# Norms and weight casts moved from VectorE to ScalarE, low parts to GpSimd, in an SSM block with a gated feed-forward part

## The chip, the cores and the metric

The kernel runs on one core of a Trainium2 chip. A core has TensorE (PE, with its weight loads, PEld, listed apart), VectorE (DVE), ScalarE (ACT), GpSimd (POOL) and SyncE (SP), which here only issues DMAs. The metric is the device time of one execution in microseconds. Before the change it is 608.14 us, the median of three runs (607.9 to 608.25).

## The reference

The input is x of shape (4, 512, 256): four batches of 512 tokens. Both halves of the block normalize x, scale and shift it by factors made from a small conditioning vector, and add their gated result to x.

```python
mod = (silu(c) @ wmod).reshape(4, 6, 1, 256)      # sa, ca, ga, sb, cb, gb
h = layernorm(x) * (1 + ca) + sa
x = x + ga * attn(h)
h = layernorm(x) * (1 + cb) + sb
x = x + gb * ffn(h)

# attn: a state-space layer, 32 heads of 8 channels, state 64, written as masked attention
proj = u @ W_in.T                                  # 4640 columns: x, B, C | z | A_log
xBC = causal_conv4(xBC) + conv_b                   # per channel, 4 taps
Lm = exp(segsum(-softplus(A_log)))                 # lower triangular decay
M = einsum('blhn,bshn,bhls->bhls', C, B, Lm)
y = einsum('bhls,bshp->blhp', M, x) + D * x
out = y * silu(z + z_bias) @ W_out.T

# ffn
hidden = fwht(silu(x @ W1.T) * (x @ W3.T))         # Walsh-Hadamard transform, 1024 wide
out = hidden @ W2.T
```

## The kernel before

**Split products.** The large products are done on float32 values held as two parts in a format of TensorE (F32R): a high part, which is the value cast to that format, and a low part, the value minus the high part. A projection (`proj`) is six matmuls, high by high, low by high and high by low, over two halves of the 256 inputs. So each weight that is loaded is split by `split`: one cast for the high part, one subtraction on POOL for the low part. The transposed activations are split in `modulate`: ACT makes the high part from PSUM, DVE makes the full value `hf` from PSUM, and a subtraction (L292) makes the low part.

**Stages.** The first part goes over eight units, two halves `i` of the heads by four batches `b`: all batches of half 0, and then of half 1. A unit has eight steps `k` (64 in all), two groups of four called `m`. Each step projects B and C for two heads (`project`: `bc` and `cc`), puts each through `conv`, builds the decay factors `l` (`prep_l`), multiplies them with the products of B and C (`attend`, L446), and transposes B (`turn_b`). For each `m`, states are summed over chunks of 64 tokens (`states`, `turn_states` with the scan L550), and `intra` and `inter` give the output. At the end of a unit comes the gate; after half 1 of a batch also the output projection, the second norm (`normalize(b, 1, ...)`, `modulate(b, 1, ...)`) and a spill of its result to memory. The feed-forward part then runs over 32 steps, eight per batch (`up`, `down`).

**One convolution.** `conv` reads a projection from PSUM in four passes: two on ACT (L375 with the fourth tap and the bias, L377 with the first tap into `cv`), two on DVE (L378, L379), and it ends with an addition on POOL (L380). The projection's PSUM tile, one of three (`ps_p`), is free once ACT and DVE have read it.

**A norm.** `normalize` takes x as four tiles of 128 tokens by 256: per tile `bn_stats` and `bn_aggr` on DVE (L269, L270), then variance plus epsilon on DVE (L271), a power of -0.5 on POOL (L272, `rs`), and four `tensor_scalar` on DVE that subtract the mean and multiply with `rs` (L274, `xn`). `xn` has a single buffer. PE transposes it (L284) for `modulate`. The first norm of a batch is part 0 of `prologue`, its `modulate` is part 1; part 2 makes the decay sums from `hf`, which the masks `dr` and `dl` are loaded from.

**The order of work.** Python runs an agenda: each function has a due time in steps (`T`), and functions are put into the program in the order of these times. For batches 1 to 3, part 0 of `prologue` is due 11.83 steps, part 1 7.06 steps ahead of the batch's first unit. SP's queue keeps that order. For the other engines, the framework plans the order when the program is built, by a simulation of times (`schedule_with_timeline_sim=True`), and may put an instruction ahead of others that come before it in the program. `with tc.issue_after(ins)` keeps what is made inside it, on the engine of `ins`, behind `ins`; `behind(...)` does this with the last instruction noted in `last` under each name given. [...] Three places make weight splits ahead of the loop (`split_quad`, `split_xz`), others in the loop (`load_quad`, `xz1`, `load_ffn`).

Of the kernel before, what the change touches and what calls it, by code (L numbers as in the profile page):

```python
# [13 lines left out]
F32 = mybir.dt.float32  # L14
F32R = mybir.dt.float32r
BF16 = mybir.dt.bfloat16
AF = mybir.ActivationFunctionType
ALU = mybir.AluOpType
# [3 lines left out]
NB, S, DM = 4, 512, 256  # L22
# [8 lines left out]
def mamba_ffn(tc, ctx, u, c_t, wmod, win_t, cw, cb, zb, dsk, wo_t, w13_t, w2_t,  # L31
              k_ident, k_reset, k_dl, k_dr, k_had, k_own, out):
    nc = tc.nc
    ve, ac, gp, pe = nc.vector, nc.scalar, nc.gpsimd, nc.tensor
# [17 lines left out]
    def after(dt, fn, *args):  # L52
        at_time(now[0] + dt, fn, *args)
# [6 lines left out]
    def work(shape, name, tag, bufs=2, dtype=F32):  # L60
        return wk.tile(shape, dtype, name=name, tag=tag, bufs=bufs)

    def mtile(shape, name):
        return ps_m.tile(shape, F32, name=name, tag="m")
# [4 lines left out]
    def load_x(which, b, src, step=4):  # L69
        t = work([128, 4, DM], f"x{which}{b}", "x", 1)  # L70
        for n in range(0, 4, step):
            nc.sync.dma_start(t[:, n : n + step], src[:, n : n + step])
        return t

    def tok_rows(ap):
        return ap.rearrange("(t p) d -> p t d", p=128)

    x_in = {0: load_x(0, 0, tok_rows(u[0]), 2)}
# [88 lines left out]
            ts.append(t)  # L167
        return ts

    def split(dst, c0, width, ts):  # L170

        for k, t in enumerate(ts):
            d = dst[:, :, k, c0 : c0 + width]
            ve.tensor_copy(d[:, 0], t)
            gp.tensor_tensor(d[:, 1], t, d[:, 0].bitcast(F32), ALU.subtract)

    wa = const.tile([128, 2, 32], F32, name="wa")
# [1 line left out]
    wxz = {}  # L179
    wo = const.tile([128, 2, 2, DM], F32R, name="wo")  # L180
    wq = {}
# [1 line left out]
    def fetch_quad(n, half, **kw):  # L183
        return fetch(win_t[:, 544 + 1024 * n : 544 + 1024 * n + 1024], 512 * half, 512, f"wq{n}", **kw)

    def split_quad(n, half, ts):
        if half == 0:
            wq[n] = work([128, 2, 2, 1024], f"wq{n}", "wq", 2, F32R)
        split(wq[n], 512 * half, 512, ts)

    def load_quad(n, half):
        split_quad(n, half, fetch_quad(n, half))
# [1 line left out]
    def fetch_xz(i, **kw):  # L194
        return fetch(win_t[:, 256 * i : 256 * i + 256], 0, 256, f"wxz{i}", **kw)

    def split_xz(i, ts):
        wxz[i] = work([128, 2, 2, 256], f"wxz{i}", "wxz", 1, F32R)
        split(wxz[i], 0, 256, ts)

    def load_wo():
        for k in range(2):
# [41 lines left out]
    last = {}  # L244
# [12 lines left out]
    def behind(*engines):  # L257
        stack = ExitStack()
        for e in engines:
            stack.enter_context(tc.issue_after(last[e].ins))  # L260
        return stack

    def normalize(b, which, x):
        mv = work([128, 4, 2], f"mv{which}{b}", "mv")
        rs = work([128, 4], f"rs{which}{b}", "rs")
        xn = work([128, 4, DM], f"xn{which}{b}", "xn", 1)
        for t in range(4):
            bs = work([128, 6], f"bs{which}{b}{t}", "bs")
            ve.bn_stats(bs, x[:, t])  # L269
            ve.bn_aggr(mv[:, t], bs)  # L270
        ve.tensor_scalar(rs, mv[:, :, 1], EPS, None, ALU.add)  # L271
        last[gp] = gp.tensor_tensor(rs, rs, neghalf, ALU.pow)  # L272
        for t in range(4):
            ve.tensor_scalar(xn[:, t], x[:, t], mv[:, t, 0:1], rs[:, t : t + 1], ALU.subtract, ALU.mult)  # L274
        return xn

    def modulate(b, which, xn):

        sh = [msc[:, 4 * which + k, b : b + 1] for k in range(2)]
        scl = [msc[:, 4 * which + 2 + k, b : b + 1] for k in range(2)]  # L280
        pts = [mtile([128, S], f"pt{which}{b}{k}") for k in range(2)]
        for t in range(4):
            for k in range(2):
                pe.transpose(pts[k][:, 128 * t : 128 * t + 128], xn[:, t, 128 * k : 128 * k + 128], ident)  # L284
        full = [work([128, S], f"hf{which}{b}{k}", "hf") for k in range(2)]
        hts = [work([128, 2, S], f"ht{which}{b}{k}", "ht", 6, F32R) for k in range(2)]
        ac.activation(hts[0][:, 0], pts[0], AF.Identity, bias=sh[0], scale=scl[0])
        for k in (1, 0):
            ve.tensor_scalar(full[k], pts[k], scl[k], sh[k], ALU.mult, ALU.add)
        ac.activation(hts[1][:, 0], pts[1], AF.Identity, bias=sh[1], scale=scl[1])  # L290
        for k in range(2):
            last[ve] = ve.tensor_tensor(hts[k][:, 1], full[k], hts[k][:, 0].bitcast(F32), ALU.subtract)  # L292
        return full, hts

    def spill(name, tiles):
# [16 lines left out]
    xns, fulls, phss, dfs = {}, {}, {}, {}  # L312

    def prologue(b, part, fill=None):
        if part == 0:
            if b not in x_in:
                x_in[b] = load_x(0, b, tok_rows(u[b]))
            xns[b] = normalize(b, 0, x_in.pop(b))
        elif part == 1:
            fulls[b], ht[0, b] = modulate(b, 0, xns.pop(b))  # L320
            htd[b] = spill(f"htd{b}", ht[0, b])
        elif part == 2:

            full = fulls.pop(b)
            pa = mtile([128, 128], f"pa{b}")
            for k in range(2):
                for t in range(4):
                    last[pe] = pe.matmul(pa[32 * t : 32 * t + 32], wa[:, k], full[k][:, 128 * t : 128 * t + 128],
                              start=(k == 0), stop=(k == 1), skip_group_check=True, tile_position=(0, 32 * t))
            e = work([128, 128], f"spe{b}", "spe", 1)  # L330
            at = work([128, 128], f"at{b}", "at", 1)
            ac.activation(e, pa, AF.Abs)
            last[ve] = ve.tensor_scalar(at, pa, 0.0, -1.0, ALU.max, ALU.mult)
            if fill:
                fill()
            ac.activation(e, e, AF.Exp, scale=-1.0)
            ac.activation(e, e, AF.Ln, bias=1.0)
            ve.tensor_tensor(at, at, e, ALU.subtract)
            phs = phss[b] = work([128, 128], f"phs{b}", "phs", 1)
            ve.tensor_tensor_scan(phs, reset, at, 0.0, ALU.mult, ALU.add)  # L340

            parts = work([128, 3, 128], f"parts{b}", "parts", 1, BF16)
            rest = work([128, 128], f"rest{b}", "at", 1)
            ve.tensor_copy(parts[:, 0], phs)
            ve.tensor_tensor(rest, phs, parts[:, 0], ALU.subtract)
            ve.tensor_copy(parts[:, 1], rest)
            last[ve] = ve.tensor_tensor(parts[:, 2], rest, parts[:, 1], ALU.subtract)
            p_dr3[b] = dram.tile([NH, 3, S], BF16, name=f"p3{b}")
            p_dr[b] = dram.tile([NH, S], F32, name=f"pd{b}")
            p_end[b] = dram.tile([NH, NC], F32, name=f"pend{b}")  # L350
            for t in range(4):
                (gp if T["p3gp"] and b == 0 and t % 2 else nc.sync).dma_start(p_dr3[b][:, :, 128 * t : 128 * t + 128], parts[32 * t : 32 * t + 32])
            after(1, write_sums, b, phs)
        elif part == 3:

            phs = phss.pop(b)
            df = dfs[b] = work([128, 128], f"df{b}", "df", 1)
            p_c = phs.rearrange("p (c l) -> p c l", l=Q)
            ve.tensor_tensor(df.rearrange("p (c l) -> p c l", l=Q), p_c[:, :, Q - 1 :].to_broadcast([128, 2, Q]),
                             p_c, ALU.subtract)  # L360
            ac.activation(df, df, AF.Exp)
        else:
            pw = mtile([128, 128], f"pw{b}")
            pe.transpose(pw, dfs.pop(b), ident)
            wdec[b] = const.tile([128, 4, NH], F32, name=f"wd{b}")
            ac.activation(wdec[b].rearrange("p t h -> p (t h)"), pw, AF.Copy)
# [6 lines left out]
    def conv(ps, tl, dst):  # L373
        w = cw_sb[:, tl]
        ac.activation(dst, ps, AF.Identity, bias=cb_sb[:, tl : tl + 1], scale=w[:, 3:4])  # L375
        v = work([128, S], "cv", "cv", 3)
        last[ac] = ac.activation(v, ps, AF.Copy, scale=w[:, 0:1])  # L377
        ve.scalar_tensor_tensor(dst[:, 1:], ps[:, : S - 1], w[:, 2:3], dst[:, 1:], ALU.mult, ALU.add)  # L378
        ve.scalar_tensor_tensor(dst[:, 2:], ps[:, : S - 2], w[:, 1:2], dst[:, 2:], ALU.mult, ALU.add)  # L379
        last[gp] = gp.tensor_tensor(dst[:, 3:], dst[:, 3:], v[:, : S - 3], ALU.add)  # L380

    units = [(i, b) for i in range(2) for b in range(NB)]
# [258 lines left out]
    q00 = fetch_quad(0, 0, **early)  # L641
    fxz = fetch_xz(0, **early)
    q01 = fetch_quad(0, 1, **early)
    q10 = fetch_quad(1, 0, **early)
    q11 = fetch_quad(1, 1)
    with behind(gp):
        split_quad(0, 0, q00)
    prologue(0, 1)
    with behind(gp):
        for t in sts:  # L650
# [3 lines left out]

    def split_more():
        with behind(gp, ve):
            split_xz(0, fxz)
            split_quad(0, 1, q01)

    prologue(0, 2, split_more)  # L660
    load_d(0)
    for k in range(AHEAD):
        for half in range(2):
            with behind(pe, ve):
                project(k, half)
        if k == 1:
            with behind(gp, ve):
                split_quad(1, 0, q10)
    with behind(pe):
        x_proj(0)  # L670
    with behind(gp, ve):
        split_quad(1, 1, q11)
    prologue(0, 3)
    with behind(pe):
# [204 lines left out]
```

## Time and profile before

| | |
|---|---|
| median of 3 runs | 608.14 us |
| profiled execution: own time, span | 611.31 us, 609.4 us |
| mean granted clock of TensorE | 0.976 |
| busy PE, DVE, ACT, POOL | 549.5, 454.3, 367.5, 314.9 us |
| xn (L274), DVE | 32 instructions, 17.7 us |
| low parts of activations (L292), DVE | 16 instructions, 13.4 us |
| casts of weights (L174), DVE | 28 instructions, 17.2 us |
| `fh` (L693), ACT, 128x512 from SBUF into F32R | 32 instructions, mean 632 ns |
| `fl` (L694), POOL, 128x512 from SBUF into F32R | 31 instructions, mean 1294 ns |

Busy times of a group are unions: two instructions that overlap count once, while a mean is of single durations. A line with an arrow at its end, such as [1.87 <-DVE bc L379], says that the engine stood idle for 1.87 us just before and that the named instruction released it. The stages in what follows are start-up (0 to 20 us), the ramp of the first unit (20 to 60), the loop over the units (to about 475), and the feed-forward part, whose first steps begin inside the end of the loop.

### The profile page before, as it was taken

To read this page: it belongs to the slowest core of one execution; us is meant where nothing else is said; L and a number is where in the kernel's file an instruction comes from. 1 tells how busy PE (TensorE), PEld (TensorE's weight loads), DVE (VectorE), ACT (ScalarE), POOL (GpSimd) and SP (SyncE) were. 2 spreads that over 40 slices of the span, in tenths; PEclk is the share of its full clock that TensorE was granted. 3 is DMA by queue.
4 is the path that set the end of the run, shared out by engine and by line. 5 is a ranking of instruction groups with operands and counts; after the bars stand their busy time and mean duration, and the time that the engine had idled before them with its cause. 6 is when DMAs were issued, how large, how long until landed. Compare 5 with 4: busy or idle time off the path is not lost. (4 is left out here: it accounts for less than half of the span.)

```text
span 609.4 us, 16345 instructions
## 1 busy us (share of the span) xinstructions
PE 549.5 (90%) x6836; PEld 435.8 (72%) x6836; DVE 454.3 (75%) x820; ACT 367.5 (60%) x600; POOL 314.9 (52%) x288
## 2 busy tenths in 40 slices
PE   3777898899889979999999899979979999999996
PEld 3554676678667756676777576757857888888886
DVE  5978798897796879889879888989888384343342
ACT  5657678867867765697785678567643233322221
POOL 5564243644534476764655558456576545325341
PEclk9978999999889989999999999999988999999999
DMA  6331111020313305201501244145139033304021
GB/s 199 107 127 70 40 37 72 10 67 3 105 27 101 110 2 164 92 3 58 170 4 37 75 131 146 58 131 176 37 119 298 9 124 117 125 0 147 1 78 36
DMA packets 42113, 52.00 MB, mean 85 GB/s; under 512 B 18230, under 2 KB 30260, under 8 KB 42040
## 3 DMA queue, kind: packets, MB, share of 16 engines
q1 hardware_dynamic: 40504, 50.54, 26.2%
q8 instruction: 54, 0.88, 0.6%
q10 hardware_dynamic: 1472, 0.38, 0.3%
q14 instruction: 19, 0.16, 0.1%
q0 software_dynamic: 64, 0.05, 0.0%
HBM read 33.51 MB, written 17.44 MB: 84 GB/s over the span
## 5 line engine op out<-in xcount | busy, mean ns | idle before, releaser
L380 POOL TENSOR_TENSOR cc<-cc,cv 128x509 f32<-128x509 f32 x64 | 70.5, 1101 | 75.2 <-DVE cc L379 69.7
L380 POOL TENSOR_TENSOR bc<-bc,cv 128x509 f32<-128x509 f32 x64 | 71.3, 1114 | 58.0 <-DVE bc L379 34.5
L242 PE MATMUL f<-h,wf 128*128 128x512 f32 x384 | 98.3, 396 | 0.0
L242 PEld LDWEIGHTS f<-h,wf 128*128 128x128 f32 x384 | 69.4, 191 | 12.3
L694 POOL TENSOR_TENSOR fl<-ft,fh 128x512 fp32r<-128x512 f32 x31 | 40.1, 1294 | 64.1 <-ACT fh L693 60.7
L375 ACT ACTIVATE cc<-pcc,cb_sb,cw_sb 128x512 f32<-128x512 f32 x64 | 49.8, 778 | 26.5 <-PE pcc L242 15.0
L375 ACT ACTIVATE bc<-pbc,cb_sb,cw_sb 128x512 f32<-128x512 f32 x64 | 50.0, 781 | 24.7 <-PE pG L255 15.2
L242 PE MATMUL pcc<-ht,wq 128*128 128x512 f32 x192 | 55.7, 428 | 10.0 <-DVE bc L379 8.1
L378 DVE SCALAR_TENSOR_TENSOR cc<-pcc,cw_sb,cc 128x511 f32<-128x511 f32 x64 | 47.4, 741 | 20.9 <-ACT cv L377 19.9
L242 PE MATMUL pbc<-ht,wq 128*128 128x512 f32 x192 | 56.7, 432 | 5.5 <-DVE cc L379 4.0
L693 ACT ACTIVATE fh<-ft 128x512 fp32r<-128x512 f32 x32 | 20.2, 632 | 66.9 <-PE pdyi L701 36.8
L689 DVE SCALAR_TENSOR_TENSOR ft<-ft,f 128x512 f32<-128x512 f32 x32 | 21.9, 687 | 49.6 <-ACT ft L688 45.4
L242 PE MATMUL pcc<-hr,wq 128*128 128x512 f32 x192 | 52.1, 405 | 3.0 <-ACT cv L377 1.5
L242 PE MATMUL pbc<-hr,wq 128*128 128x512 f32 x192 | 51.7, 404 | 2.2 <-DVE cc L379 2.0
L242 PEld LDWEIGHTS pcc<-ht,wq 128*128 128x128 f32 x192 | 37.4, 202 | 20.4 <-DVE bc L379 4.1
L454 ACT ACTIVATE bt<-bT 128x512 f32<-128x512 f32 x64 | 38.6, 604 | 19.6 <-PE bT L452 19.5
L378 DVE SCALAR_TENSOR_TENSOR bc<-pbc,cw_sb,bc 128x511 f32<-128x511 f32 x64 | 47.3, 740 | 3.0 <-ACT cv L377 3.0
L242 PEld LDWEIGHTS pbc<-ht,wq 128*128 128x128 f32 x192 | 37.2, 203 | 17.3 <-DVE cc L379 1.9
L379 DVE SCALAR_TENSOR_TENSOR bc<-pbc,cw_sb,bc 128x510 f32<-128x510 f32 x64 | 47.4, 741 | 1.2
L379 DVE SCALAR_TENSOR_TENSOR cc<-pcc,cw_sb,cc 128x510 f32<-128x510 f32 x64 | 47.4, 741 | 1.1
L452 PE MATMUL bT<-ident,bc 128*128 128x128 f32 x256 | 41.8, 286 | 3.9 <-DVE cc L379 1.2
L377 ACT ACTIVATE cv<-pcc,cw_sb 128x512 f32<-128x512 f32 x64 | 43.7, 683 | 2.0 <-POOL bc L380 2.0
(148 smaller groups left out, 1237.0 us busy)
## 6 DMA issues: line engine op xcount, KB each, us to landing
wq<-win_t SPq DMA_DIRECT2D x16, 256.0 KB
htd<-ht SPq DMA_DIRECT2D x8, 512.0 KB
hr<-htd SPq DMA_DIRECT2D x8, 512.0 KB
h2d<-ht SPq DMA_DIRECT2D x8, 512.0 KB
h<-h2d SPq DMA_DIRECT2D x8, 512.0 KB
x<-u SPq DMA_DIRECT2D x7, 512.0 KB
ex<-pd SPq DMA_DIRECT2D x8, 256.0 KB
ygd<-yg SPq DMA_DIRECT2D x4, 512.0 KB
```

What stands on the lines that cost most here:

```text
L242: last[pe] = pe.matmul(ps, w[:, a, k, c0 : c0 + 128], ht[k][:, b], start=(n == 0), stop=(n == 5))
L375: ac.activation(dst, ps, AF.Identity, bias=cb_sb[:, tl : tl + 1], scale=w[:, 3:4])
L377: last[ac] = ac.activation(v, ps, AF.Copy, scale=w[:, 0:1])
L378: ve.scalar_tensor_tensor(dst[:, 1:], ps[:, : S - 1], w[:, 2:3], dst[:, 1:], ALU.mult, ALU.add)
L379: ve.scalar_tensor_tensor(dst[:, 2:], ps[:, : S - 2], w[:, 1:2], dst[:, 2:], ALU.mult, ALU.add)
L380: last[gp] = gp.tensor_tensor(dst[:, 3:], dst[:, 3:], v[:, : S - 3], ALU.add)
L452: pe.transpose(pt[:, t], bc[:, 128 * t : 128 * t + 128], ident)
L454: ac.activation(bts[k], pt, AF.Copy)
L689: ve.scalar_tensor_tensor(t, t, 1.0, p1, ALU.add, ALU.mult)
L693: ac.activation(hi, t, AF.Copy)
L694: (ve if (b, f) == (NB - 1, 7) else gp).tensor_tensor(lo, t, hi.bitcast(F32), ALU.subtract)
```

## The change

Four edits:

1. `split` casts on ACT unless it is told to use DVE. The first half quad, the first `xz` and the second half quad (six casts) stay on DVE; the other 22 go to ACT. The two later splits of the start-up are kept behind `last[ac]`, the last `cv` pass, where they were kept behind `last[ve]`.
2. `normalize` makes `xn` on ACT with a scale `rs` and a bias `nm`, which is minus the mean times `rs`, made by one more small instruction on DVE. The first norm (batch 0) stays as it was.
3. `modulate` makes the low parts on POOL, but for batch 0's first.
4. The statistics of the first norms of batches 1 to 3 are kept behind the second DVE pass of the last convolution put into the program before them. This holds for what runs on DVE, since the noted instruction is on DVE.

```diff
-    def split(dst, c0, width, ts):
+    def split(dst, c0, width, ts, e=ac):
         for k, t in enumerate(ts):
             d = dst[:, :, k, c0 : c0 + width]
-            ve.tensor_copy(d[:, 0], t)
+            if e is ac:
+                ac.activation(d[:, 0], t, AF.Copy)
+            else:
+                ve.tensor_copy(d[:, 0], t)
             gp.tensor_tensor(d[:, 1], t, d[:, 0].bitcast(F32), ALU.subtract)
...
         last[gp] = gp.tensor_tensor(rs, rs, neghalf, ALU.pow)
+        if (b, which) == (0, 0):
+            for t in range(4):
+                ve.tensor_scalar(xn[:, t], x[:, t], mv[:, t, 0:1], rs[:, t : t + 1], ALU.subtract, ALU.mult)
+            return xn
+        nm = work([128, 4], f"nm{which}{b}", "nm")
+        ve.scalar_tensor_tensor(nm, mv[:, :, 0], -1.0, rs, ALU.mult, ALU.mult)
         for t in range(4):
-            ve.tensor_scalar(xn[:, t], x[:, t], mv[:, t, 0:1], rs[:, t : t + 1], ALU.subtract, ALU.mult)
+            ac.activation(xn[:, t], x[:, t], AF.Identity, bias=nm[:, t : t + 1], scale=rs[:, t : t + 1])
         return xn
...
+        e = ve if (which, b) == (0, 0) else gp
         for k in range(2):
-            last[ve] = ve.tensor_tensor(hts[k][:, 1], full[k], hts[k][:, 0].bitcast(F32), ALU.subtract)
+            last[e] = e.tensor_tensor(hts[k][:, 1], full[k], hts[k][:, 0].bitcast(F32), ALU.subtract)
...
-            xns[b] = normalize(b, 0, x_in.pop(b))
+            with behind(*(["conv"] if b else [])):
+                xns[b] = normalize(b, 0, x_in.pop(b))
...
-        ve.scalar_tensor_tensor(dst[:, 2:], ps[:, : S - 2], w[:, 1:2], dst[:, 2:], ALU.mult, ALU.add)
+        last["conv"] = ve.scalar_tensor_tensor(dst[:, 2:], ps[:, : S - 2], w[:, 1:2], dst[:, 2:], ALU.mult, ALU.add)
...
     with behind(gp):
-        split_quad(0, 0, q00)
+        split_quad(0, 0, q00, ve)
...
         with behind(gp, ve):
-            split_xz(0, fxz)
-            split_quad(0, 1, q01)
+            split_xz(0, fxz, ve)
+            split_quad(0, 1, q01, ve)
...
-            with behind(gp, ve):
+            with behind(gp, ac):
                 split_quad(1, 0, q10)
...
-    with behind(gp, ve):
+    with behind(gp, ac):
         split_quad(1, 1, q11)
```

## The prediction

> **What bounds the kernel now.** I read the busy times of the page, cut them into stages with the busy time by stretch, asked which PE gaps end on VectorE in each stage, and then read the timeline around the long gaps. The page first (busy us, share of the span, instructions):
>
> ```profile
> PE 549.5 (90%) x6836; PEld 435.8 (72%) x6836; DVE 454.3 (75%) x820; ACT 367.5 (60%) x600; POOL 314.9 (52%) x288
> ...
> PE 27%; DVE 12%; DMA 3%; POOL 2%; issue 1%; ACT 1%; SPq 0%; DVEq 0%; POOLq 0%
> ```
>
> The second line is the chain that ended last. It reaches back only to 328 us, and its PE share is mostly the feed-forward part at the end; before 475 us DVE is its largest member. By stage (length, then busy PE, PEld, DVE, ACT, POOL, the granted clock and DMA):
>
> ```profile
> 20.00:60.00 40.00, 28.18 (x181) 20.04 (x182) 34.39 (x69) 25.88 (x43) 21.64 (x21) 0.87 0.24 82
> 60.00:200.00 140.00, 128.06 (x2007) 97.48 (x2008) 116.33 (x220) 106.14 (x176) 60.48 (x57) 0.98 0.17 50
> 200.00:260.00 60.00, 53.46 (x853) 40.93 (x853) 50.51 (x84) 40.86 (x68) 39.22 (x35) 0.97 0.29 93
> ...
> 320.00:475.00 155.00, 141.93 (x2046) 109.31 (x2044) 134.68 (x251) 97.14 (x160) 94.00 (x84) 0.98 0.38 120
> 475.00:609.40 134.40, 129.05 (x808) 114.15 (x807) 55.33 (x91) 37.29 (x61) 53.31 (x43) 0.99 0.22 71
> ```
>
> From 475 us the kernel is PE alone (129.05 of 134.4). From 20 to 475 us (260 to 320 is not shown: PE 58.48, DVE 50.44, ACT 48.11, POOL 34.34) PE is busy 410.1 of 455, DVE 386.4 (85%), ACT 318.1 (70%), POOL 249.7 (55%). PE idles 45 us there, and by its waits in each stage some 34 us of these end on DVE. The operations that the change moves stand in those gaps. Timeline, DVE and PE:
>
> ```profile
> 31.42 4.84 DVE L274 TENSOR_SCALAR xn<-x,mv,rs 128x256 f32<-128x256 f32 x4
> ...
> 42.22 0.75 DVE L269 BATCH_NORM_STATS2 bs<-x 128x6 f32<-128x256 f32 x2 [3.08 <-DMA x<-u]
> ...
> 212.44 1.45 DVE L174 CAST wq<-wq 128x512 fp32r<-128x512 f32 x1 [0.18 <-DMA wq<-win_t]
> ...
> 214.60 2.84 PE L242 MATMUL pcc<-ht,wq 128*128 128x512 f32 x6 [1.87 <-DVE bc L379]
> ...
> 450.44 0.43 DVE L174 CAST wf<-wf 128x512 fp32r<-128x512 f32 x1 [2.06 <-DMA wf<-w_t]
> 450.78 2.32 DVE L274 TENSOR_SCALAR xn<-x,mv,rs 128x256 f32<-128x256 f32 x4
> ...
> 454.43 1.12 PE L548 MATMUL sT<-ident,st 128*128 128x128 f32 x4 [3.99 <-DVE l L446]
> ```
>
> At 31 us four normalizing instructions take 4.84 us of a DVE that the first convolutions need. At 42 us DVE stands 3.08 us for x of batch 2, whose statistics were put in front of convolutions. At 212 a cast makes `bc` late and PE waits 1.87. At 450 DVE first waits 2.06 for a weight, then normalizes, and the product `l` behind it is late: PE stands 3.99 us, the longest such gap.
>
> **What the skill says, and the trace.** The Trainium skill, "SBUF — State Buffer", section "Who interferes with whom": a VectorE copy, cast or tensor_scalar in a two-port mode, or one with two SBUF inputs, and a GpSimd instruction shut each other out; PE and ACT wait for nobody. The trace agrees, by the form (ns min/median/max):
>
> ```profile
> L274 DVE TENSOR_SCALAR xn<-x,mv,rs x32: 395/408/1691, 7.7 to 496.2; 128x256 f32<-128x256 f32 x32
> ...
> L292 DVE TENSOR_TENSOR ht<-hf,ht x16: 659/684/1760, 15.0 to 501.1; 128x512 fp32r<-128x512 f32 x16
> ...
> L174 DVE CAST wq<-wq x16: 414/852/1446, 10.7 to 248.5; 128x512 fp32r<-128x512 f32 x16
> ```
>
> The slow ones lie under POOL instructions (31.4 to 36.2 us: four xn of 1.2 to 1.4 us under POOL adds that fill the time), while the convolution passes, which read PSUM, stay at 0.74 us. So what is moved off DVE is just what suffers from POOL. "Perfetto Trace Analysis", section "Optimizing Scalar/DVE Operations", says that offloading a saturated VectorE to ScalarE may pay, and that between GpSimd and VectorE it might not, for this port; no run here shows that yet.
>
> **The change, part by part.** The base is the profiled execution: span 609.4, own time 611.31, against a median of 608.14; a gain in the span is taken over to the median unchanged.
>
> *Off DVE between 20 and 475 us*, from the busy time of each line by stage: xn 6.22 + 1.38 + 5.09 = 12.7; low parts (L292) 1.33 + 2.57 + 6.88 = 10.8; casts (L174) 1.43 + 8.12 + 4.05 = 13.6. Together 37.1 us. Added: `nm`, one for each of the six norms there; a 128x4 instruction of that kind (L271) takes 0.17 us, 0.97 when POOL has the port: 1 to 6 us, I take 2. DVE falls from 386.4 to about 351 (77%). Before 20 us nothing moves (the exceptions keep batch 0's norm, low parts and six casts); after 475 us the last norm, 2.35 + 1.29 us, is hidden under PE.
>
> *Onto ACT.* A cast costs what `fh` (L693, SBUF to fp32r 128x512) costs, 0.63 us: 20 of these, and two of 256 columns. The slope from wd (128x128, 0.278) to bt (128x512, 0.604) is 0.85 ns a column, so these are 0.41. Casts: 13.4 us. The xn with bias and scale by pointer: cc (L375, same kind, 512 columns) is 0.78, less 256 x 0.85 = 0.56. The skill's price, "ScalarE: Activation LUTs", section "What ACT_TABLE_LOAD costs", gives 280 + 0.833 x 256 + 93 = 586 ns, an estimate; I take 0.57. Six norms in the stage are 24 x 0.57 = 13.7. ACT goes from 318.1 to 345 (76%). This is hidden where ACT now waits for PE (14.3 us on `st`, 9.9 on `bt` in the last stage; at 450.9 to 456.0 it stands still). Without that cover it is up to 27 us. A norm is 2.3 us in a row, and behind it in ACT's queue stand the first conv passes; PE has three projection banks and fills one in 1.39 us, so I charge 0.5 us for each of six: 3 us.
>
> *Onto POOL.* 12 low parts in the stage at 1.29 us (fl, L694, same shape): 15.5 us, POOL to 265 (58%). Their readers are far: between `hf` of batch 2 (97.9 us) and the store of its sums (116.4) lie 18 us, and the projections come later. SP's queue already stands for L292 (81.8 us in 14 waits at the spills); behind it are the sums of the same batch and the next loads. Two low parts are 2.6 us against 1.4, plus POOL's own queue, at worst 6.3 us (its longest wait for a convolution), against those 18. I cost this at zero; without the cover it is 1 to 7 us per batch, and what is late next would be the decay mask (`dr`).
>
> *The tie.* Statistics of batches 1 to 3 now follow the second DVE pass of the last convolution put into the program before them: `xc` of batch 0, then k = 5 (at 67.9 us, the sixth L379 of `cc`) instead of 42.2, for batch 2. Its x lands by 42.2, so the wait of 3.08 (and 0.85 at 82.5) goes. xn is needed for `hf` at 97.9, thus 30 us later.
>
> *The sum, from PE's gaps.* I add only gaps whose DVE queue holds a moved instruction just before the releaser. 20 to 60 us: 0.94 (pt on xn), 1.11 (xc behind xn), 1.55 (ht behind the wait for x), 1.15, 2.97 = 7.7. 60 to 200: 0.90 + 1.17 behind xn and ht at 100 to 102 = 2.1. 200 to 260: 1.87 + 1.19 behind casts = 3.1. 320 to 475: 1.47, 0.63, 1.65 (behind an ht pair of 2.35), 3.99 = 7.7. Total 20.6. Not all closes: the next input may be late too. Bounds are half (10.3) and all; I take 0.8, because in most cases ACT and PE had long delivered: 16.5. Less 3 for ACT bursts, less 1.5 for `nm`, which still makes DVE wait for POOL's pow (about 1.1 us, as xn does now). Net 12 us: 608.1 - 12 = **596**.
>
> **Rivals.**
> *DVE is the bound throughout.* The chain gives DVE 73 us (12% of 609.4) while DVE is busy 134.7 us in the last stage: 54%. 37.1 x 0.54 = 20, plus the 3 us of the x wait: about 585. For it: DVE at 85%. Against: PE's own 410 us bound it first.
> *Gain given back to order.* Every engine's order but SP's is planned anew when the program is built, with simulated times and due times that were not changed. The gaps close and open elsewhere: 602 to 607. For it: 45 us of gaps exist now with no engine at its limit.
> *ACT blocks (slower).* xn waits on ACT for statistics, pow on POOL, and `nm`. If it is planned before its inputs are really there, ACT's queue, with the conv passes that free PE's banks, stands. POOL holds a pow up to 6.3 us behind an add. The 16.5 us are gone at 2.75 us of PE idle for each of six norms; at 4 us it ends at 608 + 24 - 16.5 = 616. Against: xn waited for rs only 4.3 us in four waits, the longest 1.2.
> *The tie does nothing* (statistics already behind those convolutions): excluded for batch 2 by the times above; it would take 3 us from the gain.
>
> **Chances.** My forecast (590 to 602) 0.58; DVE bound (below 590) 0.12; given back (602 to 606.9) 0.12; no change 0.03; ACT blocks 0.15. A difference under 0.2% (1.2 us) can hardly be told. Faster 0.82, same 0.03, slower 0.15. The range 586 to 610 leaves out one part in ten above and less below.
>
> **What would show it.** DVE 20 to 475 near 350 us; no xn, cast or low part of 1 us or more left on DVE after 20 us; stage gains of about 5 us in the ramp and 5 between 320 us and the start of the feed-forward part, which stays at 133 to 135; the gaps of 3.99, 2.97 and 1.87 gone. It is wrong if ACT shows long waits before xn (L274) or casts, if PE's gaps then end on ACT, or if POOL's low parts hold up the spills until `dr` is late.

## The result, and the profile after

The changed kernel takes **598.48 us** (median of four runs, 596.91 to 600.72), against 608.02 us for the kernel before in the same comparison: a ratio of **0.9841, 95% interval 0.9814 to 0.9868**, so 9.5 us faster. The forecast was 596, 12 us faster, with a range of 586 to 610. The profiled execution took 600.72 us, its span is 598.8 (before: 609.4), its mean granted clock 0.976 as before. Both profiled executions are slower than the medians, by 3.2 us (before) and 2.2 us, and the four runs of the changed kernel alone lie 3.8 us apart; so a difference of about 2 us between two whole traces is not read as an effect of an edit. All times in this document are of undisturbed executions; the kernel with second norms only on ACT (below) was profiled in a disturbed one (2311.54 us, its other five 597.17 to 605.19), so it has times but no trace to read.

The page, busy times and the chain that ended last:

```profile
PE 550.4 (92%) x6836; PEld 436.1 (73%) x6836; DVE 419.3 (70%) x763; ACT 389.5 (65%) x650; POOL 329.0 (55%) x302
...
PE 31%; DVE 8%; ACT 2%; POOL 2%; issue 1%; DMA 1%; POOLq 0%; DVEq 0%
```

DVE lost 35 us and is now 8% of the chain instead of 12. By stage, with the columns of before (stretch, length, busy PE, PEld, DVE, ACT, POOL, granted clock, DMA share, GB/s). The feed-forward part is again taken as the last 134.4 us, from 464.4:

```profile
20.00:60.00 40.00, 33.08 (x264) 23.94 (x262) 29.20 (x59) 35.05 (x60) 23.70 (x22) 0.87 0.25 85
60.00:200.00 140.00, 130.99 (x2067) 99.56 (x2066) 118.47 (x222) 108.75 (x185) 69.90 (x65) 0.99 0.18 55
200.00:250.00 50.00, 45.73 (x724) 34.67 (x723) 36.45 (x65) 40.32 (x70) 35.29 (x32) 1.00 0.31 96
250.00:310.00 60.00, 58.57 (x898) 44.95 (x898) 50.62 (x83) 48.82 (x82) 35.62 (x34) 1.00 0.20 60
310.00:464.40 154.40, 142.00 (x2033) 109.75 (x2032) 119.64 (x225) 103.94 (x175) 96.11 (x87) 0.96 0.38 119
464.40:598.80 134.40, 129.28 (x811) 114.16 (x809) 52.40 (x86) 40.09 (x66) 56.07 (x45) 0.99 0.22 73
```

From 20 us to the feed-forward part PE does the same work (410.4 us, before 410.1) in 444.4 us instead of 455: its idle time fell from 45 to 34 us. The feed-forward part did not change: from the first `fh` to the end it is 140.9 us before and 140.2 now. The moved instructions, by form (ns min/median/max, first and last start, shape):

```profile
L283 ACT ACTIVATE xn<-x,nm,rs x28: 585/588/605, 38.7 to 487.4; 128x256 f32<-128x256 f32 x28
...
L175 ACT ACTIVATE wq<-wq x12: 618/631/709, 25.8 to 234.8; 128x512 fp32r<-128x512 f32 x12
...
L302 POOL TENSOR_TENSOR ht<-hf,ht x14: 1268/1278/1464, 42.9 to 494.5; 128x512 fp32r<-128x512 f32 x14
...
L281 DVE SCALAR_TENSOR_TENSOR nm<-mv,rs x7: 144/161/165, 37.6 to 485.8; 128x4 f32<-128x4 f32 x7
```

Where the 10 us were won is best read from a common milestone: the end of the first convolution pass of `cc` on ACT (L375, now L387) of each step `k`. Times in us, changed minus before:

| step | 4 | 8 | 12 | 16 | 24 | 28 | 36 | 44 | 48 | 52 | 56 | 63 | first `fh` |
|---|---|---|---|---|---|---|---|---|---|---|---|---|---|
| | -5.9 | -6.9 | -10.5 | -7.1 | -9.2 | -11.8 | -12.4 | -12.4 | -11.8 | -8.7 | -6.8 | -6.8 | -9.9 |

The forecast's whole 12 us are there by step 36 (258.8 us, before 271.3), half of them already by step 4. Then the second half of the loop gives back 5.6 us between steps 44 and 56 (306 to 396 us), and wins 3 again at the end. The forecast had +5 us for this stretch.

What happens there, in the timeline (start, duration, engine, instruction, and the idle time before it with its releaser), all engines:

```profile
326.94 2.08 ACT L283 ACTIVATE xn<-x,nm,rs 128x256 f32<-128x256 f32 x4 [1.85 <-DVE nm L281]
...
331.94 1.72 PE L575 MATMUL pi<-cc,sts 128*32 128x64 f32 x56 [2.88 <-POOL sts L566]
...
382.63 0.78 ACT L387 ACTIVATE cc<-pcc,cb_sb,cw_sb 128x512 f32<-128x512 f32 x1
...
384.43 2.08 ACT L283 ACTIVATE xn<-x,nm,rs 128x256 f32<-128x256 f32 x4 [1.02 <-DMA ex<-pd]
...
386.42 0.75 ACT L387 ACTIVATE bc<-pbc,cb_sb,cw_sb 128x512 f32<-128x512 f32 x1
...
387.65 0.67 ACT L389 ACTIVATE cv<-pcc,cw_sb 128x512 f32<-128x512 f32 x1
387.78 0.75 DVE L390 SCALAR_TENSOR_TENSOR bc<-pbc,cw_sb,bc 128x511 f32<-128x511 f32 x1 [2.18 <-ACT cv L389]
...
388.85 1.85 PE L233 MATMUL hd<-w2b,had 128*128 128x512 f32 x2 [2.31 <-ACT bt L466]
```

These are the second norms of batches 0 and 1 (in the changed kernel L283 is `xn`, L387 and L389 are the convolution's passes on ACT, L390 and L391 those on DVE; other kernels have line numbers of their own). At 383.4 ACT has done the first pass for `cc`; then it stands 1.02 us, for `nm` too, which ends at 384.40, spends 2.08 on four `xn`, and only at 386.42 begins the passes of `bc`. The second pass for `cc`, which reads a product that was complete when the first began at 382.63, comes at 387.65: it stood behind the `xn` while ACT did nothing. DVE waits 2.18 us for what stands behind, PE 2.31. At 327 ACT stands 1.85 us for `nm` first, and PE stands 2.88 us. Before the change there was no PE gap above 1.5 us at either place.

### The profile page after: what moved, and what is told of

Same layout as the page of the kernel before. It is cut to its first block, busy times and chain, and to the rows that moved or that the text cites. A ratio compares the mean times of both kernels' runs of the same rounds, so it can differ in the third digit from the quotient of the medians.

```text
span 598.8 us, 16340 instructions
## 1 busy us (share of the span) xinstructions
PE 550.4 (92%) x6836; PEld 436.1 (73%) x6836; DVE 419.3 (70%) x763; ACT 389.5 (65%) x650; POOL 329.0 (55%) x302
## 5 line engine op out<-in xcount | busy, mean ns | idle before, releaser
L392 POOL TENSOR_TENSOR bc<-bc,cv 128x509 f32<-128x509 f32 x64 | 69.9, 1092 | 56.3 <-DVE bc L391 28.3
L390 DVE SCALAR_TENSOR_TENSOR cc<-pcc,cw_sb,cc 128x511 f32<-128x511 f32 x64 | 47.6, 744 | 35.2 <-ACT cv L389 35.2
L387 ACT ACTIVATE bc<-pbc,cb_sb,cw_sb 128x512 f32<-128x512 f32 x64 | 50.0, 781 | 21.1 <-PE pG L258 15.7
L387 ACT ACTIVATE cc<-pcc,cb_sb,cw_sb 128x512 f32<-128x512 f32 x64 | 50.2, 784 | 19.9 <-PE pcc L245 14.8
L245 PE MATMUL pcc<-hr,wq 128*128 128x512 f32 x192 | 54.1, 417 | 1.4 <-DVE bc L391 0.7
L390 DVE SCALAR_TENSOR_TENSOR bc<-pbc,cw_sb,bc 128x511 f32<-128x511 f32 x64 | 47.5, 743 | 10.7 <-ACT cv L389 10.4
L391 DVE SCALAR_TENSOR_TENSOR bc<-pbc,cw_sb,bc 128x510 f32<-128x510 f32 x64 | 47.6, 743 | 1.3
L391 DVE SCALAR_TENSOR_TENSOR cc<-pcc,cw_sb,cc 128x510 f32<-128x510 f32 x64 | 47.5, 742 | 1.2
L258 PEld LDWEIGHTS pG<-cc,bc 64*64 64x64 f32 x2048 | 34.5, 135 | 13.5 <-issue 7.9
L389 ACT ACTIVATE cv<-pbc,cw_sb 128x512 f32<-128x512 f32 x64 | 44.2, 691 | 0.0
```

Source lines behind the costliest of these rows:

```text
L245: last[pe] = pe.matmul(ps, w[:, a, k, c0 : c0 + 128], ht[k][:, b], start=(n == 0), stop=(n == 5))
L258: self.before = pe.matmul(*args, **kw)
L391: last["conv"] = ve.scalar_tensor_tensor(dst[:, 2:], ps[:, : S - 2], w[:, 1:2], dst[:, 2:], ALU.mult, ALU.add)
```

## The experiments

The prediction's theory is that the value of each part is the load that it takes off DVE (less what it puts on ACT), called the load theory here. Its rivals: ACT blocks at the norms (the burst theory in the expectations); the tie is more than the 3 us that it was priced at (the ramp theory); and the planner's order, built anew for any edit, gives and takes a few us by itself (the planner theory). Of each edit only the deciding lines are shown. Each ratio is to the kernel before on the same chip (medians 609.44, 610.14 and 609.62 us in the three groups), with its 95% interval; a hundredth is 6.1 us.

### Each part alone

The tie alone (edit 4):

```diff
-            xns[b] = normalize(b, 0, x_in.pop(b))
+            with behind(*(["conv"] if b else [])):
+                xns[b] = normalize(b, 0, x_in.pop(b))
```

> The kernel before with the tie of the statistics alone. Load theory (VectorE time taken off pays about in proportion to the gaps it stood in): the waits for x of 3.1 and 0.8 us go and 3 us of statistics leave the ramp, 2 to 3 us faster, 605.5. Ramp theory (most of the gain is the order of the first 60 us): 4 to 6 us faster, about 603, and the lead is there by step k = 8. Planner theory (any edit reshuffles all queues): anywhere within 4 us of before, with the lead lost or won at stages where nothing was changed.

The casts alone (edit 1):

```diff
-            ve.tensor_copy(d[:, 0], t)
+            if e is ac:
+                ac.activation(d[:, 0], t, AF.Copy)
```

> The kernel before with the 22 weight casts on ScalarE and nothing else. Load theory: the gaps behind casts (1.87, 1.19 and most of 3.99) close, 4 to 5 us faster, 603.5, won between k = 24 and 32 and after k = 56. Ramp theory: 1 us. Planner theory: within 4 us either way, not at those places.

The norms alone (edit 2):

```diff
-            ve.tensor_scalar(xn[:, t], x[:, t], mv[:, t, 0:1], rs[:, t : t + 1], ALU.subtract, ALU.mult)
+            ac.activation(xn[:, t], x[:, t], AF.Identity, bias=nm[:, t : t + 1], scale=rs[:, t : t + 1])
```

> The kernel before with xn of seven norms on ScalarE and nothing else. Load theory: 7 us of gaps less 4.5 us of bursts on ScalarE and nm, 2 to 4 us faster, 605. Ramp theory: most of the single gains, since four xn take 4.8 us of VectorE at 31 us: 4 to 5 us faster, won by k = 8. Planner theory: within 4 us either way.

The low parts alone (edit 3):

```diff
-            last[ve] = ve.tensor_tensor(hts[k][:, 1], full[k], hts[k][:, 0].bitcast(F32), ALU.subtract)
+            last[e] = e.tensor_tensor(hts[k][:, 1], full[k], hts[k][:, 0].bitcast(F32), ALU.subtract)
```

> The kernel before with the low parts of seven transposed tiles on GpSimd and nothing else. Load theory: about 3 us of gaps (1.65, 0.9 and part of the ramp), 2 us faster, 606. Port theory (GpSimd gets 18 us more and shuts out xn and casts that are still on VectorE): no gain or up to 3 us slower, and more xn and casts of over 1 us. Planner theory: within 4 us either way.

### Each part left out

The changed kernel with one part undone: no tie, no casts, no norms, no low parts.

```diff
-            with behind(*(["conv"] if b else [])):
-                xns[b] = normalize(b, 0, x_in.pop(b))
+            xns[b] = normalize(b, 0, x_in.pop(b))
```

> The changed kernel without the tie. Load theory: 2 to 3 us slower than the changed kernel, 601. Ramp theory: most of the 6 us won by k = 4 is lost, 603. Planner theory: within 4 us of the changed kernel, either way.

```diff
-            if e is ac:
-                ac.activation(d[:, 0], t, AF.Copy)
-            else:
-                ve.tensor_copy(d[:, 0], t)
+            ve.tensor_copy(d[:, 0], t)
```

> The changed kernel with all weight casts back on VectorE. Load theory: 4 to 5 us slower, 603, lost between k = 24 and 32 and after k = 56. Ramp theory: 1 us slower. Planner theory: within 4 us either way.

```diff
-            ac.activation(xn[:, t], x[:, t], AF.Identity, bias=nm[:, t : t + 1], scale=rs[:, t : t + 1])
+            ve.tensor_scalar(xn[:, t], x[:, t], mv[:, t, 0:1], rs[:, t : t + 1], ALU.subtract, ALU.mult)
```

> The changed kernel with xn of all norms back on VectorE. Load theory: 2 to 4 us slower, 601.5. Burst theory (the give-back of 5 us between k = 48 and 56 is xn on ScalarE, in the second norms): lost in the ramp, but that stretch is 3 to 5 us shorter, in sum equal. Planner theory: within 4 us either way.

```diff
-            last[e] = e.tensor_tensor(hts[k][:, 1], full[k], hts[k][:, 0].bitcast(F32), ALU.subtract)
+            last[ve] = ve.tensor_tensor(hts[k][:, 1], full[k], hts[k][:, 0].bitcast(F32), ALU.subtract)
```

> The changed kernel with the low parts back on VectorE. Load theory: 2 us slower, 600.5. Pool theory (sts and conv additions wait behind low parts on GpSimd, so that the loss between k = 48 and 56 comes from them): 2 us faster or equal, 597. Planner theory: within 4 us either way.

Measured, with the worth of the part in us (a minus is a gain; in the last column its ratio with all four parts, 0.9841, less that without it):

| part | alone | worth | without it | worth in the whole |
|---|---|---|---|---|
| tie | 0.9909 [0.9878, 0.9940] | -5.5 | 1.0006 [0.9988, 1.0025] | -10.0 |
| casts | 0.9909 [0.9876, 0.9942] | -5.5 | 0.9908 [0.9882, 0.9935] | -4.1 |
| norms | 1.0087 [1.0059, 1.0115] | +5.3 | 0.9746 [0.9720, 0.9772] | +5.8 |
| low parts | 0.9996 [0.9980, 1.0012] | -0.2 | 0.9805 [0.9780, 0.9831] | +2.2 |

By these numbers the load theory missed for the tie (it expected 2 to 3 us, alone and in the whole), for the norms (it expected a gain) and for the low parts (2 us alone, a loss of 2 when taken back); only the casts have the size that it expected (4 to 5 us), though not the places. The ramp theory's size for the tie alone, 4 to 6 us by step 8, was met. The last column sets kernels of two comparisons side by side, each by its own ratio; its values are known to about 2 us either way, so the low parts' +2.2 is not clear of zero.

**The tie** carries the change: without it, the three parts that take 37 us off DVE give nothing. The timeline of the kernel without the tie, DVE, PE and ACT:

```profile
42.06 0.75 DVE L272 BATCH_NORM_STATS2 bs<-x 128x6 f32<-128x256 f32 x2 [5.42 <-DMA x<-u]
...
45.04 2.90 PE L245 MATMUL pbc<-ht,wq 128*128 128x512 f32 x6 [7.03 <-DVE mv L273]
...
48.49 0.16 DVE L281 SCALAR_TENSOR_TENSOR nm<-mv,rs 128x4 f32<-128x4 f32 x1 [2.21 <-POOL rs L275]
...
48.74 2.08 ACT L283 ACTIVATE xn<-x,nm,rs 128x256 f32<-128x256 f32 x4 [3.08 <-issue]
```

The x of batch 2 ends DVE's wait at 42.06; before the change it did so at 42.22. A less loaded DVE is at its statistics 2.5 us sooner (36.6 us instead of 39.1) and waits 5.42 us instead of 3.08. In the other three kernels without the tie the wait ends at 42.60 (casts alone), 42.66 (norms alone) and 41.76 (low parts alone), after 4.39, 5.05 and 3.07 us: the sooner DVE gets there, the longer it stands. The convolutions behind it are late, PE stands 7.03 us, and the norm that now runs on ACT comes straight after. By step 4 this kernel is 7.9 us behind the changed one, and 8.0 behind at every milestone from step 28 to the last: the loss is made there. The casts alone and the norms alone show the same, with PE gaps of 5.04 us at 44.06 and 5.46 us at 44.83: at step 3 they are 5.5 and 5.2 us ahead of the kernel before, at step 4 they are 1.0 and 2.4 behind. The tie also moves the statistics of batch 1, from 24.2 to 30.7 us in the kernel with the tie alone; what that is worth was not separated.

**The casts** are worth 4 to 5.5 us, alone and in the whole. Alone, the milestones stand at -2.2 us at step 24 and at -5.9 at step 28, the stretch of the casts of the next weights: the gap of 1.87 us is gone, and so are the 3.41 us at half the granted clock that followed it (last section). After step 56, where the load theory had the rest, nothing is won: -6.5 us there, -6.2 at the first `fh`, since one of 2.41 us stands in place of the gap of 3.99, and one of 1.98 at 402. In the whole the loss without the casts lies in the ramp (1.4 us by step 4) and after step 63 (3.7 us).

**The norms** cost 5 us, alone and in the whole, although they take 12.7 us off DVE. Alone they make the gaps of the changed kernel at the same two places, which is against the planner theory: PE in the kernel with the norms alone:

```profile
344.71 0.31 PE L569 MATMUL pi<-cc,sts 128*32 128x64 f32 x6 [2.95 <-POOL sts L560]
...
400.47 0.70 PE L230 MATMUL hd<-w2b,had 128*128 128x512 f32 x1 [2.29 <-ACT bt L460]
```

With the norms back on DVE, in the kernel without that part, the second of these places reads:

```profile
379.65 1.38 DVE L277 TENSOR_SCALAR xn<-x,mv,rs 128x256 f32<-128x256 f32 x4 [0.91 <-POOL rs L275]
...
380.39 0.69 ACT L382 ACTIVATE cv<-pcc,cw_sb 128x512 f32<-128x512 f32 x1
...
381.69 0.66 PE L553 MATMUL sT<-ident,st 128*128 128x128 f32 x4 [0.62 <-DVE l L451]
```

DVE waits 0.91 us for `rs` and spends 1.38 us; ACT meanwhile makes its passes, and PE stands 0.62 us. This kernel, at **594.92 us (0.9746)**, is faster than the kernel before and the changed one.

### Which norms, the low parts in company, and the planner's own spread

The tie and the casts without the other two (edits 1 and 4), so that the low parts can be judged without the norms:

```diff
-        last[e] = e.tensor_tensor(hts[k][:, 1], full[k], hts[k][:, 0].bitcast(F32), ALU.subtract)
+        last[ve] = ve.tensor_tensor(hts[k][:, 1], full[k], hts[k][:, 0].bitcast(F32), ALU.subtract)
...
-        ac.activation(xn[:, t], x[:, t], AF.Identity, bias=nm[:, t : t + 1], scale=rs[:, t : t + 1])
+        ve.tensor_scalar(xn[:, t], x[:, t], mv[:, t, 0:1], rs[:, t : t + 1], ALU.subtract, ALU.mult)
```

> The kernel before with the tie and the casts on ScalarE; xn and low parts stay on VectorE. Order theory (the tie pays, xn on ScalarE costs, low parts on GpSimd give nothing): at least as fast as the changed kernel without xn, ratio to before 0.970 to 0.978. Load theory (VectorE time is what pays, xn only suffers from its place): 0.982 to 0.986, the sum of the two parts alone, since 24 us go back to VectorE.

The changed kernel with ACT making `xn` for first norms only:

```diff
-        if (b, which) == (0, 0):
+        if which == 1 or (b, which) == (0, 0):
```

> The changed kernel with xn on ScalarE for the first norms of batches 1 to 3 only; xn of the four second norms stays on VectorE. If the second norms carry the cost of xn on ScalarE (it is planned ahead of convolution passes and waits for nm): equal to the kernel with no xn on ScalarE, 0.974 to 0.977, and the PE gaps of 2.9 and 2.3 us at steps k = 48 and 56 are gone. If the cost lies in all norms: 0.979 to 0.981.

And for second norms only:

```diff
-        if (b, which) == (0, 0):
+        if which == 0:
```

> The changed kernel with xn on ScalarE for the four second norms only. If the second norms carry the cost: equal to the changed kernel, 0.982 to 0.985, with both gaps there. If the cost lies in all norms: 0.978 to 0.980.

The changed kernel with one due time moved a little, which changes no work:

```diff
-gate_z=5.89
+gate_z=5.85
```

> The changed kernel with one due time moved from 5.89 to 5.85 steps, so that the gate's z projection of each unit comes into the program half a projection earlier; no work is moved between engines. Load and order theories: within 2 us of the changed kernel, 0.982 to 0.987. Planner theory (any edit is worth 4 us either way): outside of 0.980 to 0.989.

| kernel | ratio | median |
|---|---|---|
| tie and casts | 0.9856 [0.9834, 0.9879] | 600.63 us |
| norms on ACT, first only | 0.9765 [0.9744, 0.9787] | 595.37 us |
| norms on ACT, second only | 0.9836 [0.9797, 0.9876] | 599.28 us |
| due time moved | 0.9872 [0.9850, 0.9893] | 601.62 us |

**The cost of the norms lies in the second ones.** With first norms alone on ACT the kernel is as fast as with none (0.9765 and 0.9746, overlapping); with second norms alone it is as slow as the changed kernel. The milestones of the changed kernel against the first of these stand at a constant +3.0 us from step 28 to 44 and go to +8.6 at step 56: 5.6 us for two norms, 2.8 us each. The two PE gaps are gone in its trace, and the clock is 1.00 there. The kernel with second norms only has no trace to read, so that it has the two gaps is not shown.

The other traces bear this out, and split the 5.6 us. The stretch from step 44 to 56, by who makes the `xn` of the second norms:

| kernel | second norms on | two longest PE gaps, us | us at half clock | stretch, us |
|---|---|---|---|---|
| before; tie; casts; low parts; without norms; tie and casts; first norms only | DVE | 1.5, 1.2 | 0 | 84.0 to 84.1 |
| without low parts | ACT | 3.01, 2.31 | 0 | 86.0 |
| norms alone | ACT | 2.95, 2.29 | 3.4 | 87.4 |
| without casts | ACT | 2.99, 2.32 | 3.4 | 87.7 |
| due time moved | ACT | 3.29, 1.31 | 6.8 | 87.7 |
| changed; without tie | ACT | 2.9, 2.3 | 10.2 | 89.7 |

Wherever the second norms are on ACT the stretch is longer, and nowhere else. With the same two gaps and no loss of clock it is 1.9 us longer, about 1 us for each norm; what comes on top, up to 3.7 us, goes with the time at half clock. This also answers the pool theory, by which low parts on POOL make the loss: the kernel without them met its expectation (2 us faster or equal), but it has both gaps at full length, and only the clock differs.

**An edit without work: within 2 us.** The moved due time gave 0.9872, which is 1.9 us more than the changed kernel by the ratios, whose intervals overlap, and 1.6 by the spans (600.4, 598.8), less than the 3.8 us between runs of the changed kernel. The planner did put its engines' work into another order from about 64 us on, and in between its milestones were up to 4.2 us behind. So the 2.2 us that the changed kernel would win without its low parts are not told apart from order or from noise.

**The low parts are worth something where the second norms stay on DVE.** With norms on DVE, the tie and casts give 0.9856, and with the low parts on POOL too 0.9746: 6.7 us, or 5.2 us by the spans (598.2, 593.0), and the intervals do not overlap. The order theory's expectation was missed, the load theory's met, but not by less idle time: from 20 us to the first `fh` PE idles 33.2 us with the low parts on DVE and 33.7 with them on POOL. The difference is in PE's busy time (404.8 and 399.0 us for the same work), with 27.3 and 17.1 us at half clock. One place of the kernel with tie and casts:

```profile
395.57 2.35 DVE L295 TENSOR_TENSOR ht<-hf,ht 128x512 fp32r<-128x512 f32 x2
...
397.84 0.73 DVE L383 SCALAR_TENSOR_TENSOR cc<-pcc,cw_sb,cc 128x510 f32<-128x510 f32 x1
398.63 2.37 PE L245 MATMUL pbc<-hr,wq 128*128 128x512 f32 x6 [1.87 <-DVE cc L383]
```

A pair of low parts takes 2.35 us on DVE, where two undisturbed ones are 1.37 (0.686 each by its median), the convolution's last pass stands behind it, and PE waits 1.87 us. With low parts on POOL this gap is not there; nearby is one of 1.25 us. Between steps 56 and 60 (392 to 421 us) the milestones of the two kernels move 1.5 us further apart. They do so at two more places, by 1.1 us between steps 4 and 8 (50 to 78) and by 1.6 between 16 and 20 (133 to 158). At each of the three the kernel with low parts on DVE has 3.4 us more at half clock (from 44, 154 and 399 us), worth up to 1.7 us each. Low parts run on DVE at 147 us too, but also at 91 to 94 and at 340, where nothing moves; only the place at 395 was followed to a PE gap. So that the low parts cost these clock losses is shown at one place at most, and why the same move gives nothing alone (0.9996) is not settled.

## Why the prediction was right, and where its terms were not

**The work moved: right.** From 20 us to the feed-forward part DVE fell from 386.4 to 354.4 us (forecast about 351), ACT rose from 318.1 to 336.9 (345), POOL from 249.7 to 260.6 (265). The prices held: `xn` on ACT 588 ns (taken 570; the estimate from the Trainium skill, "ScalarE: Activation LUTs", section "What ACT_TABLE_LOAD costs", was 586), casts 631 and 416 ns (630 and 410), low parts 1278 ns (1290). `nm` took 0.16 us each time, so 1 us, not the 2 taken for all. No `xn`, cast or low part is left on DVE after 20 us. The prediction quotes the Trainium skill, "SBUF — State Buffer", section "Who interferes with whom", without one condition: a VectorE instruction with two SBUF inputs contends with a GpSimd instruction that reads SBUF. POOL's additions and subtractions here do read it, so the reading stands.

**The base, that gain comes only out of PE's gaps: right for this pair of kernels.** PE's work stayed at 410 us and its idle time fell by 11 us (forecast 12). That PE's busy time is the same in both rests on an equal time at half clock in the two traces, 27.3 us between 20 us and the feed-forward part; with first norms only on ACT it is 13.7 us, and from 20 us to the first `fh` PE is busy 398.4 us, not 404.5, at nearly the same idle time (32.7 and 34.0). The rival in which DVE is the bound throughout (585) fell. Of the three gaps named, 1.87 is gone. The one of 2.97 before `pcc` of step 4 is still 2.48, now for another DVE instruction (`dx`, at 46.42); the ramp's gain came from its smaller gaps. In place of 3.99 there is one of 2.53.

**By stage the sum was right only in total, and that is in part luck.** Ramp: forecast about 5, measured 5.9 by step 4. From there to step 36: 2 were left in the sum, measured 6.5. From there to the feed-forward part: forecast 5, measured a loss of 2.5 (5.6 given back, 3.1 won in the last gap). By what ended PE's waits (over 0.15 us) from 20 us to the first `fh`: those that end on DVE fell from 34.3 to 17.0 us, 17.3 less where the sum (16.5 less 1.5 for `nm`) had 15; those that end on ACT or POOL rose from 5.7 to 12.9, 7.2 more where it had 3. Two of the prediction's own signs of being wrong came true: ACT stands up to 1.85 us before `xn`, and PE's gaps of 2.31 and 2.53 us end on ACT. Two terms were mis-sized, in opposite directions:

1. **"I charge 0.5 us for each of six" norms on ACT.** The second norms of batches 0 and 1 cost 2.8 us each in this trace, about 1 us of it as wait and the rest with the clock, while the first norms cost nothing that shows. This is the mechanism of the rival "ACT blocks", near the 2.75 us that it named as its break-even, but at two of the six norms, so that it took 5.6 us and not 16.5. The charge rested on PE's three projection banks; it left out that `xn` is put into ACT's queue ahead of passes which DVE and PE already wait for, and stands there for `nm`, and it left out the clock (below). With first norms only on ACT the change would have ended 4.6 us lower (0.9765).
2. **The tie "would take 3 us from the gain".** It is worth 5.5 us alone and 10 in the change. The 3.08 us wait was counted as a fixed loss. But it ends when a DMA lands, between 41.8 and 42.7 us in all five kernels without the tie, so time saved ahead of it only lengthens it. The gaps of the ramp, of which the sum puts two down to `xn` and only one to this wait, could close only with the tie: the other three parts alone stand at +1.0, +2.4 and +0.2 us at step 4, the tie alone at -5.7.

**The casts: right at one place, low in size** (3.1 us of gaps, times 0.8, is 2.5; measured 4.1 to 5.5). At the gap of 1.87 alone 3.7 us were won between steps 24 and 28, about the gap and half of the 3.41 us at half clock behind it. **Low parts: their move to POOL, costed at zero, shows no cost alone; in company it gains** 5 to 7 us with the second norms on DVE, and with norms on ACT nothing that can be told. The spills never made `dr` late: the only PE gap over 1 us on it is in the ramp, 3.15 us (before 3.77).

**"Gain given back to order" (602 to 607)** fell as a cause for the whole: an edit without work moved the span by 1.6 us, which is not clear of noise. The single parts sum to -5.9 us and the whole is -9.7, on the same base, so measured prices of single parts could not have been added up to the result.

## What to carry to other kernels

A wait for a transfer that lands at a time of its own swallows what is saved ahead of it on that engine; move the waiting instruction first, then lighten the engine. Work put on an engine with spare time costs what stands behind it in the queue, not its busy time: here 2.08 us of `xn` cost about 1 us of waiting, and with the clock up to 2.8, where conv passes were next, and nothing elsewhere, so it pays to move only the instances that have cover. Test parts one at a time and left out one at a time: the four here were worth -5.5, -5.5, +5.3 and 0 alone, and the two best kernels (0.9746 and 0.9765) were the change without one of them and without half of it.

## What was not expected of the hardware

**A PE gap can cost again in the clock, by where it falls in time.** Granted clock (the column after POOL; PE's busy time is the first after the length) around the changed kernel's two gaps at the second norms, of 2.88 and 2.31 us:

```profile
327.68:331.09 3.41, 1.18 (x10) 0.56 (x8) 3.31 (x6) 3.41 (x7) 2.73 (x4) 1.00 0.10 26
331.09:337.92 6.83, 5.98 (x71) 5.13 (x72) 3.98 (x6) 3.83 (x7) 3.97 (x4) 0.50 0.01 4
385.71:389.12 3.41, 1.10 (x10) 0.62 (x9) 1.34 (x2) 3.41 (x7) 0.00 (x0) 1.00 0.00 0
389.12:392.53 3.41, 3.41 (x46) 1.91 (x49) 3.41 (x6) 2.61 (x5) 2.40 (x3) 0.50 0.00 0
```

and in the kernel without low parts, around its gaps of 3.01 and 2.31 us at the same places:

```profile
327.28:330.70 3.42, 1.85 (x15) 1.04 (x13) 2.80 (x5) 3.42 (x7) 2.17 (x3) 1.00 0.37 114
330.70:334.11 3.41, 1.76 (x62) 1.62 (x63) 3.41 (x7) 3.26 (x7) 2.10 (x3) 1.00 0.03 7
334.11:337.52 3.41, 3.41 (x19) 2.62 (x18) 3.11 (x5) 2.79 (x5) 2.68 (x3) 1.00 0.00 0
385.31:388.72 3.41, 1.75 (x18) 0.89 (x22) 3.18 (x5) 3.41 (x8) 1.00 (x1) 1.00 0.01 2
388.72:392.14 3.42, 3.42 (x70) 2.95 (x63) 2.57 (x4) 1.93 (x4) 2.82 (x3) 1.00 0.44 98
```

The changed kernel loses half of its clock for 6.83 and for 3.41 us, the other one keeps it. Where PE sets the pace, half of such a time is lost on top of the gap: at most 3.4 and 1.7 us here.

What decides can be read from the traces. In each of the 13 that can be read (the two kernels compared and eleven variants) the clock is either 1.00 or 0.50 and, once the loop runs, changes only on a grid of 3.41 us, which lies differently in each trace. Taking every stretch of the grid at full clock, from 25 us after the start to 25 us before the end: of 60 in which PE was busy for 50% or less, all 60 are followed by a stretch at half clock; of 17 with 51 to 55%, 4; of 1912 with more, none. So a gap of 2.3 us halves the clock when most of it lies in one stretch (above: busy 1.10 of 3.41 us), and not when the grid cuts it or the work around it fills enough (1.75 of 3.41). Even 1.87 us was enough in the kernel before (at 214.60, busy 1.54 of 3.41), and gaps of 3.01 and 2.29 us were not (without low parts; norms alone, at 400.47). The Trainium skill, "TensorE: Matmul & The Clock Gate", section "Part 1: The HAM clock gate (the "warmup" mystery)", has the half clock after at least one idle window of about 3.4 us; the length agrees with the grid, but here a stretch need not be idle, only busy for less than about half. PE's busy times are partly modelled, so the border is known no better than to a few per cent.

A sum over PE's gaps, as in the prediction, leaves this out, for closing gaps as for opening them. Whether a given gap of 2 to 3 us is paid for twice depends on where the grid lies, and the mean granted clock of the changed kernel's four runs does differ, from 0.976 to 0.982.
